# Both layernorms by way of DRAM and VectorE's block turns instead of TensorE's transposes

## The chip, the cores and the metric

The kernel runs on one core of one Trainium2 chip. The metric is the time of one execution in device microseconds; runs of the same kernel are compared by their medians.

## What is computed

There are eight batches of 1024 tokens, each with a width of 512, and a context of 1024 rows with a width of 384. Each batch passes through two blocks, both gated with tanh of a scalar and added to x:

```python
x = x + tanh(g_xattn) * xattn(layernorm(x), ctx)     # 8 heads of 64, softmax over 1024 context rows
x = x + tanh(g_ffn)   * ffn(layernorm(x))            # 16 heads of 32, self attention

# ffn, per head
q_norm = q / norm(q);  q_scaled = (q_norm + query_embedding) * softplus(temperature)
h = softmax(q_scaled @ k.T / sqrt(32)) @ v
# gates: softmax of 15 routed logits, the top 3 kept; softmax of 2 shared logits
out = (h * sum_of_gates) @ Wp.T + bp

def layernorm(x):      # over the 512 of a row, without weights
    return (x - mean(x)) / sqrt(var(x) + 1e-5)
```

Both layernorms work along a row of x. The projections after them contract over these 512, so TensorE needs the normalised rows turned: features on the partitions, tokens along the free axis.

## The kernel before

Everything is in float32, but for copies of queries and keys in bfloat16 from which the row maxima are taken. A batch is 8 tiles of 128 tokens. A chunk is 128 of the 512 columns of the heads: 2 heads in the first attention and 4 in the second, so each attention has 4 chunks. A chunk's life is: project q and k (`pq`, `pk`, and in the second attention `pn` for the norm of q), take the row maxima (TensorE writes `pm`, VectorE reduces to `mx`), turn the maxima (`pr`), cast them on ScalarE (`rows`), copy them with four small DMAs into one row (`sh`), and then go step by step through the keys: scores `sc` on TensorE, exp on ScalarE into `e`, pair sums of `e` on GpSimd (L483), sums of the pairs on VectorE (L496) or, where VectorE is late, on TensorE (`sum`, L516), and values `av` on TensorE.

The order on TensorE, ScalarE, VectorE and GpSimd is written by hand: a small planner in the kernel keeps a clock `at` for TensorE, VectorE and GpSimd, adds assumed costs with `pe(...)`, `dve(...)` and `pool(...)`, and decides from it which work goes between the steps of an attention. `attend` runs one chunk's attention, and takes as fillers what belongs to other chunks or to the next batch. The order of DMAs on the queue of SyncE (SP) is left to the framework's scheduler; the queue is served in that order, and a DMA that waits holds those behind it.

The layernorms are these steps of it:

- Batch 0's first layernorm stands at the kernel's start (`norm` and `transposed`).
- For the next batch, `stats1` (L750) is a filler of the attention over the last chunk of the first attention: for each of 8 tiles it loads x (`xs`) and takes mean and variance on VectorE (`bn_stats`, `bn_aggr`), and after the eighth it makes the reciprocal deviations of all tiles at once on ScalarE (Ln, Exp).
- `ln1` (L759) is a filler of the attention over chunk 2 of the second attention: it loads x again (`xn`), scales it in place on ScalarE (L203), transposes it with four matmuls against the identity into PSUM (`pt`, L218), and ScalarE copies that to `y1T` (L219).
- `between` (L944) stands between the two attentions: for each tile the output projection of the first attention (`po`, 16 matmuls of the program), the gated residual on VectorE (L955), statistics, Ln, Exp and the scaled row (`norm`, L205), and, two tiles behind, the same transposes and copy into `y2T`. GpSimd adds the bias of the last projection to x (L961). The last two transposes stand behind the first three quarters of the next chunk's q projection. That projection and the one of k are taken in halves of 512 tokens; the second half reads tiles 4 to 7.

The tag `wa` has four buffers of a tile (128x512), which loaded rows and scaled rows share.

Of the kernel before, what the change touches and what calls it, by code (L numbers as in the profile page):

```python
# [10 lines left out]
F32 = mybir.dt.float32  # L11
# [5 lines left out]
P = 128  # L17
# [4 lines left out]
def tile_gated_block(  # L22
# [38 lines left out]
    nc = tc.nc  # L61
    B, N, D = x.shape
    DC = cT.shape[1]
    NT = N // P
    ND = D // P
# [14 lines left out]
    epool = ctx.enter_context(tc.tile_pool(name="epool", bufs=9))  # L80
    work = ctx.enter_context(tc.tile_pool(name="work", bufs=2))
    small = ctx.enter_context(tc.tile_pool(name="small", bufs=1))
    ps_gen = ctx.enter_context(tc.tile_pool(name="ps_gen", bufs=3, space=bass.MemoryType.PSUM))
    ps_sc = ctx.enter_context(tc.tile_pool(name="ps_sc", bufs=2, space=bass.MemoryType.PSUM))
    ps_av = ctx.enter_context(tc.tile_pool(name="ps_av", bufs=1, space=bass.MemoryType.PSUM))
# [17 lines left out]
    def load_w(ap, name):  # L103

        k, m = ap.shape
        w = wpool.tile([P, k // P, m], F32, tag="wbig", name=name)
        nc.sync.dma_start(out=w, in_=ap.rearrange("(c p) m -> p c m", p=P))
        return w
# [79 lines left out]
    def inverse(rs, mv):  # L188

        nc.scalar.activation(rs, mv[..., 1:2], AF.Ln, bias=eps_c)  # L190
        nc.scalar.activation(mv[..., 1:2], rs, AF.Exp, scale=-0.5)
        nc.vector.scalar_tensor_tensor(
            mv[..., 0:1], mv[..., 0:1], -1.0, mv[..., 1:2], ALU.mult, ALU.mult
        )

    def stats(mv, xt, key):
        st = small.tile([P, 6], F32, tag="st", name=f"st_{key}", bufs=2)
        nc.vector.bn_stats(st, xt)
        nc.vector.bn_aggr(mv, st)
        dve(1000)  # L200

    def scaled(xn, xt, mv):
        nc.scalar.activation(xn, xt, AF.Identity, bias=mv[:, 0:1], scale=mv[:, 1:2])  # L203

    def norm(xt, key):  # L205

        mv = small.tile([P, 2], F32, tag="mv", name=f"mv_{key}", bufs=2)
        rs = small.tile([P, 1], F32, tag="rs", name=f"rs_{key}", bufs=2)
        xn = work.tile([P, D], F32, tag="wa", name=f"xn_{key}", bufs=4)
        stats(mv, xt, key)  # L210
        inverse(rs, mv)
        scaled(xn, xt, mv)
        return xn

    def transposed(xn, yT, t, key):
        pt = ps_gen.tile([P, ND, P], F32, tag="gen", name=f"pt_{key}_{t}")
        for c in range(ND):
            nc.tensor.transpose(pt[:, c, :], xn[:, ts(c, P)], ident)  # L218
        nc.scalar.copy(yT[:, :, ts(t, P)], pt)  # L219
        pe(TR)  # L220
# [3 lines left out]
    WIDE, MM, PAIR, FOUR, TR, SUM, EXP = 700, 950, 300, 350, 800, 1000, 2100  # L224

    part = [False]
# [7 lines left out]
    def pe(ns):  # L234
        at["PE"] += ns

    def dve(ns):
        at["DVE"] = max(at["DVE"], at["PE"]) + ns

    def pool(ns):  # L240
        at["POOL"] = max(at["POOL"], at["PE"]) + ns
# [18 lines left out]
    def gen(name):  # L260
        return ps_gen.tile([P, H], F32, tag="gen", name=name)
# [394 lines left out]
    def beside(a, b, n=1):  # L656

        while a or b:
            for g in [a] * n + [b]:
                if g and next(g, "end") == "end":  # L660
                    a, b = (None if g is a else a), (None if g is b else b)
                elif g:
                    yield

    def run(g, ns):

        end = at["PE"] + ns
        while g and at["PE"] < end:
            if next(g[0], "end") == "end":
                g.pop(0)  # L670
# [74 lines left out]
    def load_rows(st, t, key):  # L745
        xt = work.tile([P, D], F32, tag="wa", name=f"{key}_{st.b}_{t}", bufs=4)
        nc.sync.dma_start(out=xt, in_=x[st.b, ts(t, P), :])
        return xt

    def stats1(st):  # L750

        st.mv = small.tile([P, NT, 2], F32, tag="mv1", name=f"mv1_{st.b}")
        for t in range(NT):
            stats(st.mv[:, t, :], load_rows(st, t, "xs"), f"1_{st.b}_{t}")
            yield
        rs = small.tile([P, NT, 1], F32, tag="rs1", name=f"rs1_{st.b}")
        inverse(rs, st.mv)

    def ln1(st, xts):  # L759

        st.yT = big.tile([P, ND, N], F32, tag="yT", name=f"y1T_{st.b}")
        scaled(xts[0], xts[0], st.mv[:, 0, :])
        for t in range(NT):
            if t + 1 < NT:
                scaled(xts[t + 1], xts[t + 1], st.mv[:, t + 1, :])
            if t + 2 < NT:
                xts.append(load_rows(st, t + 2, "xn"))
            if t == 0:
                yield
            transposed(xts[t], st.yT, t, f"1_{st.b}")  # L770
            yield

    def begin(b):
# [47 lines left out]
    def out_project(ps, hT, w, t):  # L821
        part = hT[t // NQ]
        return product(ps, lambda k: part[:, k, ts(t % NQ, P)], lambda k: w[:, k, :], ND)
# [120 lines left out]
    def between(st, nxt):  # L944

        b = st.b
        wo = st.w
        st.yT = big.tile([P, ND, N], F32, tag="yT", name=f"y2T_{b}")
        xns = {}

        def output(t):
            ps = gen(f"po1_{b}_{t}")
            for _ in out_project(ps, st.hT, wo, t):
                pass
            nc.vector.scalar_tensor_tensor(st.x[t], ps, tg1, st.x[t], ALU.mult, ALU.add)  # L955
            xns[t] = norm(st.x[t], f"2_{b}_{t}")
            dve(900)

        def turn(t):
            transposed(xns.pop(t), st.yT, t, f"2_{b}")  # L960
            nc.gpsimd.tensor_tensor(st.x[t], st.x[t], bp_b, ALU.add)  # L961
            pool(1270)

        one, two, three = st.chunks[2][0:3]
        one.loads()
        two.loads()
        for t in range(NT):
            output(t)
            due(at["PE"] if t + 1 < NQ else 1e12)
            if t > 1:  # L970
                turn(t - 2)
        st.wv = load_w(wv2, f"wv2_{b}")
        st.v2 = new_v(st, 2)
        fill = [one.project(st)]
        run(fill, 3 * MM)
        three.loads()
        turn(NT - 2)
        turn(NT - 1)
        run(fill, 1e9)
        fill = [two.project(st), v2(st)]  # L980
        if nxt:
            fill.append(fetch(nxt, wv1, "wv1"))
        fill.append(three.project(st))
        run(fill, 2 * MM)
        pace(one, fill, two, 64 * MM)
        run(fill, 1e9)
        new_hT(st, 2)
# [25 lines left out]
    st = begin(0)  # L1013
    one = st.chunks[1]
# [8 lines left out]
    fill, values = [one[0].project(st)], [v1(st)]  # L1023
    run(fill, 2 * NDC * MM)
    xn = None
    for t in range(NT):
        was, xn = xn, norm(st.x[t], f"1_0_{t}")
# [9 lines left out]
    fill = values + [one[1].project(st), one[2].project(st)]  # L1037
# [4 lines left out]
    for b in range(B):  # L1042
        nxt = begin(b + 1) if b + 1 < B else None
        st.v = st.v1
        new_hT(st, 1)
        one, two = st.chunks[1], st.chunks[2]

        fill, cost = [], 0
        if prev:
            one[2].loads()  # L1050
            fill, cost = [finish(prev, one[2].project(st))], 58 * MM
        attend(one[0], one[1], b == 0, fill, cost, one[1], one[2], rate=1.4)
        one[3].loads()
        st.w = load_w(wo1, f"wo1_{b}")
        attend(one[1], one[2], False, [one[3].project(st)], 15 * MM, one[2], one[3], rate=3)
        if nxt:
            nxt.ct = load_ctx(b + 1)
        attend(one[2], one[3], False, [residual(st)], 2800, one[3])
        attend(one[3], None, False, [stats1(nxt)] if nxt else [], 2800)
        between(st, nxt)  # L1060

        st.v = st.v2
        fill = [v1(nxt)] if nxt else []
        attend(two[0], two[1], True, fill, 24.5 * MM, two[1], two[2], rate=1)
        two[3].loads()
        rows = [load_rows(nxt, t, "xn") for t in range(2)] if nxt else []
        attend(two[1], two[2], False, [two[3].project(st)], 18.5 * MM, two[2], two[3], rate=1.6 if nxt else 3)
        st.w = load_w(wp2, f"wp2_{b}")
        if nxt:
            one = nxt.chunks[1]  # L1070
            one[0].loads()
            fill = [ln1(nxt, rows), one[0].project(nxt)]
            next(fill[0])
            attend(two[2], two[3], False, fill, 8 * 2100 + 14.5 * MM, two[3], one[0], rate=1, least=2100)
            one[1].loads()
            attend(two[3], one[0], False, [one[1].project(nxt)], 14.5 * MM, one[0], one[1], rate=1)
            prev, st = st, nxt
        else:
            attend(two[2], two[3], False, [], 0, two[3])
            fill = [finish(st)]  # L1080
            attend(two[3], None, False, fill, 20 * MM, since=0.5)
# [37 lines left out]
```

## Time and profile before

| | us |
|---|---|
| median of 3 runs | 4942.89 |
| the runs | 4939.43 to 4947.75 |
| the profiled execution | 4944.07 |
| its span (first to last instruction) | 4942.1 |

| engine | busy, us | share of the span |
|---|---|---|
| TensorE (PE) | 4805.1 | 97% |
| VectorE (DVE) | 3097.8 | 63% |
| GpSimd (POOL) | 2578.9 | 52% |
| ScalarE (ACT) | 2307.4 | 47% |

The mean granted TensorE clock is 0.993. The batches follow each other in a fixed rhythm: the second batch's output loop (`between`) begins at 866.46 us, the third's at 1476.91 and the fourth's at 2088.43, so a batch takes about 611 us.

The lines from the profile are read like this. A row of the groups has the line, engine and operation, then output from inputs by the program's names, the shapes and the number of instructions; after the bar come the busy time in us (the union, so that matmuls that overlap count once) and the mean length of one in ns; after the second bar, how long the engine was idle just before these, and what ended that. A row of the timeline has the start and the length in us, then the same names; the bracket is the idle time before it and its releaser. The profile counts a float32 matmul as two instructions, a transpose as one. PEld is the loading of weights, which runs beside PE; SPq is the queue of SyncE.

### The profile page before, as it was taken

How to read it: one execution, taken by the hardware profiler on the slowest of the kernel's cores; microseconds unless marked ns; L12 is line 12 of the kernel's file. 1: busy time of each engine (PE TensorE's matmuls, PEld its weight loads, DVE VectorE, ACT ScalarE, POOL GpSimd, SP SyncE). 2: the span in 40 equal slices, each digit the busy share in tenths (PEclk: the TensorE clock that was granted, in tenths of full speed). 3: DMA queues.
4: the chain of work that ended last, by engine and by line, in shares of the span. 5: the costliest groups of instructions: out<-in, count | busy, mean ns of one | idle time of the engine just before them, and what ended most of it. 6: DMA issues, size and time to landing. Idle time of an engine off the chain costs nothing.

```text
span 4942.1 us, 83648 instructions
## 1 busy us (share of the span) xinstructions
PE 4805.1 (97%) x35564; PEld 1457.5 (29%) x35564; DVE 3097.8 (63%) x4126; ACT 2307.4 (47%) x3029; POOL 2578.9 (52%) x1346
## 2 busy tenths in 40 slices
PE   9999999999999999999999999999999999999998
PEld 2222332223322233222332223322233222333232
DVE  4557665577555765557655577555775557754664
ACT  3435634356343563436634356343662436624364
POOL 1635646366363663636636366363663636636474
PEclk9999999999999999999999999999999999999999
DMA  2010010100101001010020100101001010010000
GB/s 80 27 33 15 26 50 26 33 17 23 50 26 37 14 23 51 26 37 14 24 65 12 37 14 24 65 12 37 14 24 67 9 37 18 13 52 1 27 1 18
DMA packets 126277, 145.14 MB, mean 29 GB/s; under 512 B 14544, under 2 KB 75984, under 8 KB 125904
## 3 DMA queue, kind: packets, MB, share of 16 engines
q1 hardware_dynamic: 125616, 139.81, 8.9%
q8 instruction: 278, 4.55, 0.4%
q14 instruction: 95, 0.78, 0.1%
q10 hardware_dynamic: 288, 0.00, 0.0%
HBM read 122.47 MB, written 16.78 MB: 28 GB/s over the span
## 4 chain that ended last, share of the span: by engine, by line
PE 81%; DVE 11%; issue 2%; ACT 2%; POOL 2%; DMA 0%; SPq 0%; DVEq 0%; ACTq 0%; POOLq 0%
PE sc L467 21%; PE av L565 18%; PE po L249 8%; PE pq L249 8%; PE pm L380 7%; PE pk L249 7%; PE pv L249 5%; DVE mx L404 4%; DVE mx L421 4%; PE sum L516 3%; DVE e L496 3%; POOL e L483 1%; PE pt L218 1%; PE pn L249 1%; ACT e L478 1%
## 5 line engine op out<-in xcount | busy, mean ns | idle before, releaser
L483 POOL TENSOR_TENSOR e<-e,e 128x1024 f32<-128x1024 f32 x764 | 1864.3, 2455 | 1135.2 <-PE av L565 659.7
L478 ACT ACTIVATE e<-sc 128x1024 f32<-128x1024 f32 x1536 | 1491.4, 1021 | 1199.1 <-PE sc L467 1151.8
L421 DVE TENSOR_REDUCE mx<-pm 128x1 f32<-128x512 f32 x2332 | 1489.9, 685 | 792.2 <-PE pm L380 751.2
L467 PE MATMUL sc<-q,k 32*128 32x512 f32 (+1 forms) x6144 | 1189.9, 604 | 0.0
L496 DVE TENSOR_TENSOR e<-e,e 128x1024 f32<-128x1024 f32 x455 | 874.2, 1935 | 335.2 <-POOL e L483 334.3
L565 PE MATMUL av<-e,v 128*32 128x512 f32 (+1 forms) x6144 | 1083.0, 614 | 0.0
L380 PE MATMUL pm<-kb,qb 32*128 32x512 bf16 (+1 forms) x3072 | 625.7, 383 | 58.6 <-DVE mx L421 25.9
L404 DVE TENSOR_REDUCE mx<-pm 128x2 f32<-128x1024 f32 x370 | 427.7, 1219 | 292.5 <-PE pm L380 292.5
L467 PEld LDWEIGHTS sc<-q,k 32*128 32x128 f32 (+1 forms) x6144 | 478.5, 189 | 198.5 <-issue 186.6
L467 PE MATMUL sc<-sh,ones_b 1*128 1x512 bf16 x3072 | 406.9, 385 | 32.3 <-ACT e L478 17.3
L380 PEld LDWEIGHTS <-qb 32*128 32x128 bf16 (+1 forms) x3072 | 151.7, 92 | 918.5 <-issue 903.9
L565 PEld LDWEIGHTS av<-e,v 128*32 128x32 f32 (+1 forms) x6144 | 193.9, 117 | 609.1 <-issue 589.7
L249 PE MATMUL pq<-y1T,wq 128*32 128x512 f32 (+1 forms) x1568 | 247.1, 600 | 6.5 <-ACT r L540 2.6
L249 PE MATMUL pq<-y2T,wq 128*32 128x512 f32 x2048 | 247.5, 601 | 2.8 <-ACT rn L347 2.8
L249 PE MATMUL pv<-wv,y2T 128*32 128x512 f32 x2048 | 241.3, 597 | 0.0
L249 PE MATMUL pk<-y2T,wk 128*32 128x512 f32 x2048 | 241.2, 594 | 0.0
L249 PE MATMUL po<-wp,h2T 128*64 128x512 f32 (+1 forms) x1152 | 231.1, 595 | 0.0
L249 PE MATMUL po<-wo,h1T 128*32 128x512 f32 x2048 | 229.7, 594 | 1.2 <-ACT y2T L219 0.8
L467 PEld LDWEIGHTS <-ones_b 1*128 1x128 bf16 x3072 | 104.6, 91 | 394.2 <-issue 378.0
L249 PE MATMUL pk<-ctx,wk 128*32 128x512 f32 (+1 forms) x1176 | 189.8, 606 | 19.5 <-DMA ctx<-in_ctx 6.0
L349 POOL TENSOR_TENSOR qq<-qq,rn 128x512 f32<-128x512 f32 x64 | 89.3, 1396 | 223.3 <-ACT rn L348 215.6
L552 POOL TENSOR_TENSOR h1T<-h1T,r 128x512 f32<-128x512 f32 x64 | 81.2, 1269 | 221.5 <-ACT r L541 134.6
(109 smaller groups left out, 2985.9 us busy)
## 6 DMA issues: line engine op xcount, KB each, us to landing
x<-in_x SPq DMA_DIRECT2D x64, 256.0 KB
out<-x SPq DMA_DIRECT2D x64, 256.0 KB
xs<-in_x SPq DMA_DIRECT2D x56, 256.0 KB
xn<-in_x SPq DMA_DIRECT2D x56, 256.0 KB
ctx<-in_ctx SPq DMA_DIRECT2D x7, 1536.0 KB
wq<-in_L_xattn_Wq SPq DMA_DIRECT2D x32, 256.0 KB
wo<-in_L_xattn_Wo SPq DMA_DIRECT2D x8, 1024.0 KB
wk<-in_L_ffn_Wk SPq DMA_DIRECT2D x32, 256.0 KB
```

Of the source, the lines that this page charges most:

```text
L249: nc.tensor.matmul(ps[ts(j, w), :], lhsT=lhsT[:, ts(j, w)], rhs=rhs, start=start, stop=stop)
L349: nc.gpsimd.tensor_tensor(self.qq, self.qq, rn, ALU.mult)
L380: nc.tensor.matmul(ps, lhsT=self.qb[ts(i, width), ts(c, P)], rhs=self.kb[ts(i, width), ts(kh, H)], start=True, stop=True,)
L404: nc.vector.tensor_reduce(out, tiles[u], AX.X, ALU.max)
L421: nc.vector.tensor_reduce(mx[:, i * NT + c, kh : kh + 1], ps, AX.X, ALU.max)
L467: nc.tensor.matmul(pss[u][:, j % 2, :], lhsT=lhsT, rhs=rhs, start=(m == 0), stop=(m == 1))
L478: nc.scalar.activation(e[u], pss[u], AF.Exp)
L483: nc.gpsimd.tensor_tensor(one, one, two, ALU.add)
L496: nc.vector.tensor_tensor(accs[-1], accs[-1], a, ALU.add)
L516: nc.tensor.matmul(ps[ts(2 * u + j, self.width), :], lhsT=ones[:, 0 : self.width], rhs=acc[n][:, j, :], start=(n == 0), stop=(n == len(acc ...
L552: engine.tensor_tensor(hT, hT, r, ALU.mult)
L565: nc.tensor.matmul(self.av[ts(i, width), :], lhsT=st.v[:, kc, ts(self.c * self.nh + i, width)], rhs=e[j // 2][:, j % 2, :], start=(kc == 0 ...
```

## The change

The normalised rows no longer go through TensorE. `scaled` writes a row with its columns regrouped: the four blocks of 32 columns that belong on the same 32 partitions stand side by side. `put` stores that tile in DRAM (256 KB, one DMA). `get` loads it back with four DMAs, one for each group of 32 partitions, so that every 32 by 32 block lies on the partitions it belongs on (each piece is 512 bytes long). `turned` then has VectorE transpose all sixteen blocks in one instruction and write them to `y1T` or `y2T`.

For the first layernorm, `put1` takes the place of `stats1`: it is in the same attention, and does the whole normalisation there, with Ln, Exp and scaled row for each tile on ScalarE. `ln1` only loads (three tiles ahead) and turns; the second loading of x is gone. The filler's assumed cost goes from 2100 ns a tile to 300, and its steps now alternate with the steps of the next chunk's projection.

For the second layernorm, `between` stores each tile behind its output, loads it behind the next tile's output, and turns it three tiles behind instead of two. The last three turns stand between the first products of the next projection. The loaded tiles lie in `wa` and in two buffers that the attention uses for sums (`part`, `r`). Batch 0's first layernorm stays as it was.

```diff
+    far = ctx.enter_context(tc.tile_pool(name="far", bufs=1, space=bass.MemoryType.DRAM))
...
-    def norm(xt, key):
+    def norm(xt, key, apart=False):
...
-        scaled(xn, xt, mv)
+        if apart:
+            q = P // 32
+            scaled(
+                xn.rearrange("p (q c j) -> p q c j", q=q, c=ND),
+                xt.rearrange("p (c q j) -> p q c j", q=q, c=ND),
+                mv,
+            )
+        else:
+            scaled(xn, xt, mv)
         return xn
+
+    def put(xt, key, bufs):
+        y = far.tile([P, D], F32, tag=f"y{bufs}", name=f"y_{key}", bufs=bufs)
+        nc.sync.dma_start(out=y, in_=norm(xt, key, apart=True))
+        return y
+
+    def get(y, key, tag="wa"):
+        q = P // 32
+        xb = work.tile([P, D], F32, tag=tag, name=f"xb_{key}", bufs=4 if tag == "wa" else 1)
+        src = y.rearrange("(u i) (q f) -> q i u f", i=32, q=q)
+        for j in range(q):
+            nc.sync.dma_start(
+                out=xb[ts(j, 32), :].rearrange("i (u f) -> i u f", u=q), in_=src[j]
+            )
+        return xb
+
+    def turned(xb, yT, t):
+        nc.vector.transpose(
+            yT[:, :, ts(t, P)].rearrange("p c (u i) -> p u c i", i=32),
+            xb.rearrange("p (u c j) -> p u c j", c=ND, j=32),
+        )
+        dve(600)
...
-    def stats1(st):
-        st.mv = small.tile([P, NT, 2], F32, tag="mv1", name=f"mv1_{st.b}")
+    def put1(st):
+        st.far = []
         for t in range(NT):
-            stats(st.mv[:, t, :], load_rows(st, t, "xs"), f"1_{st.b}_{t}")
+            st.far.append(put(load_rows(st, t, "xs"), f"1_{st.b}_{t}", NT))
             yield
-        rs = small.tile([P, NT, 1], F32, tag="rs1", name=f"rs1_{st.b}")
-        inverse(rs, st.mv)
-    def ln1(st, xts):
+    def ln1(st):
+        xbs = []
+        def fetched():
+            t = len(xbs)
+            if t < NT:
+                xbs.append(get(st.far[t], f"1_{st.b}_{t}"))
+        for _ in range(3):
+            fetched()
+        yield
         st.yT = big.tile([P, ND, N], F32, tag="yT", name=f"y1T_{st.b}")
-        scaled(xts[0], xts[0], st.mv[:, 0, :])
         for t in range(NT):
-            if t + 1 < NT:
-                scaled(xts[t + 1], xts[t + 1], st.mv[:, t + 1, :])
-            if t + 2 < NT:
-                xts.append(load_rows(st, t + 2, "xn"))
-            if t == 0:
-                yield
-            transposed(xts[t], st.yT, t, f"1_{st.b}")
+            turned(xbs[t], st.yT, t)
+            fetched()
             yield
...
-        xns = {}
+        xns, xbs = {}, {}
...
-            xns[t] = norm(st.x[t], f"2_{b}_{t}")
+            xns[t] = put(st.x[t], f"2_{b}_{t}", 4)
...
-            transposed(xns.pop(t), st.yT, t, f"2_{b}")
+            turned(xbs.pop(t), st.yT, t)
...
+        tags = ("wa", "part", "wa", "r")
         for t in range(NT):
             output(t)
             due(at["PE"] if t + 1 < NQ else 1e12)
-            if t > 1:
-                turn(t - 2)
+            if t:
+                xbs[t - 1] = get(xns.pop(t - 1), f"2_{b}_{t - 1}", tags[t % 4])
+            if t > 2:
+                turn(t - 3)
+        xbs[NT - 1] = get(xns.pop(NT - 1), f"2_{b}_{NT - 1}", tags[0])
         st.wv = load_w(wv2, f"wv2_{b}")
         st.v2 = new_v(st, 2)
         fill = [one.project(st)]
-        run(fill, 3 * MM)
+        run(fill, 2 * MM)
         three.loads()
-        turn(NT - 2)
-        turn(NT - 1)
+        for t in range(NT - 3, NT):
+            turn(t)
+            run(fill, 3 * MM)
         run(fill, 1e9)
...
-        attend(one[3], None, False, [stats1(nxt)] if nxt else [], 2800)
+        attend(one[3], None, False, [put1(nxt)] if nxt else [], 2800)
...
-        rows = [load_rows(nxt, t, "xn") for t in range(2)] if nxt else []
...
-            fill = [ln1(nxt, rows), one[0].project(nxt)]
-            next(fill[0])
-            attend(two[2], two[3], False, fill, 8 * 2100 + 14.5 * MM, two[3], one[0], rate=1, least=2100)
+            turns = ln1(nxt)
+            next(turns)
+            fill = [beside(turns, one[0].project(nxt))]
+            attend(two[2], two[3], False, fill, NT * 300 + 14.5 * MM, two[3], one[0], rate=1)
```

## The prediction

> **What bounds the kernel now.** I read the page first: busy times, chain, clock.
>
> ```profile
> PE 4805.1 (97%) x35564; PEld 1457.5 (29%) x35564; DVE 3097.8 (63%) x4126; ACT 2307.4 (47%) x3029; POOL 2578.9 (52%) x1346
> ...
> PE 81%; DVE 11%; issue 2%; ACT 2%; POOL 2%; DMA 0%; SPq 0%; DVEq 0%; ACTq 0%; POOLq 0%
> ```
>
> TensorE is busy 97% and carries 81% of the chain; its clock row is 9s throughout. Only 4942.1 - 4805.1 = 137 us of the span are free of matmuls. So a change gains where it takes matmuls out, and loses where it makes the matmul queue wait. Next, the groups with shapes kept apart, for what is removed and for the nearest relative of what is added:
>
> ```profile
> L218 PE MATMUL pt<-ident,xn 128*128 128x128 f32 x512 | 83.6, 286 | 8.3 <-DVE mx L421 3.5 <-ACT part L529 2.7 <-ACT xn L203 1.7
> ...
> L198 DVE BATCH_NORM_STATS2 st<-xs 128x6 f32<-128x512 f32 x56 | 37.7, 673 | 0.0
> ...
> L219 ACT COPY y2T<-pt 128x512 f32<-128x512 f32 x64 | 36.5, 570 | 1.3
> ```
>
> All 512 transposes together are 83.6 us of PE; 480 go (the first layernorm of batch 0 keeps its 32). Then the timeline of three stages of one batch; here the second layernorm's output loop:
>
> ```profile
> 1476.91 10.51 PE L249 MATMUL po<-wo,h1T 128*32 128x512 f32 x96
> ...
> 1487.35 1.08 PE L516 MATMUL sum<-e,ones 128*64 128x512 f32 x4
> ...
> 1501.07 0.66 PE L218 MATMUL pt<-ident,xn 128*128 128x128 f32 x4
> ...
> 1501.65 3.64 PE L249 MATMUL po<-wo,h1T 128*32 128x512 f32 x32
> ...
> 1505.22 0.66 PE L218 MATMUL pt<-ident,xn 128*128 128x128 f32 x4
> ...
> 1509.52 0.75 DVE L955 SCALAR_TENSOR_TENSOR x<-po,tg,x 128x512 f32<-128x512 f32 x1 [1.70 <-PE po L249]
> ...
> 1512.01 0.81 ACT L203 ACTIVATE xn<-x,mv 128x512 f32<-128x512 f32 x1 [0.23 <-DVE mv L192]
> ```
>
> A tile with a transpose takes 1505.22 - 1501.07 = 4.15 us, without (1487.35 - 1476.91) / 3 = 3.48. From the residual add's start to the scaled row's end is 12.82 - 9.52 = 3.30 us. In the attention that hides the first layernorm's statistics:
>
> ```profile
> 1457.89 0.40 PE L467 MATMUL sc<-sh,ones_b 1*128 1x512 bf16 x4
> ...
> 1459.45 1.94 ACT L478 ACTIVATE e<-sc 128x1024 f32<-128x1024 f32 x2 [2.17 <-PE sc L467]
> ```
>
> ScalarE idles 2.17 us in a 4.11 us step here (1462.00 starts the next), and is done at 1461.39, 0.6 to 0.8 us before the next scores write the second tile that it read. That is all the room there is. Last, what a round trip costs (SyncE's queue), and what a late transfer costs:
>
> ```profile
> 693.22 0.34 SPq L894 DMA_DIRECT2D out<-x  x1
> 695.23 0.33 SPq L89 DMA_DIRECT2D x<-in_x  x1
> ```
>
> ```profile
> 511.76 2.70 SPq L436 DMA_DIRECT2D sh<-rows  x4
> ...
> 514.87 0.39 PE L467 MATMUL sc<-sh,ones_b 1*128 1x512 bf16 x1 [0.65 <-DMA sh<-rows]
> ...
> 515.54 0.37 PE L467 MATMUL sc<-sh,ones_b 1*128 1x512 bf16 x1 [0.29 <-DMA sh<-rows]
> ```
>
> The load that waits for the store is issued 2.01 us after it: a 256 KB store lands in that. The fourth of the small copies starts at 511.76 + 3 x 0.68 = 513.80 and PE goes on at 515.54: 1.74 us from issue to use. The profiled execution took 4944.07 us (span 4942.1 and 2.0 around it), 1.2 over the median of 4942.89.
>
> **The change, stage by stage.** *Second layernorm (8 batches).* Out of the PE order go two transposes behind the loop (1512.68 to 1513.93, 1.25 us) and six in it (0.67 each). VectorE gets 8 block turns a batch. None is in the trace. Nearest row: the statistics, 128x512 f32 out of SBUF, 0.67 to 0.69; below, 0.48 (the plain tensor-scalar over 128x512, L161); above, 1.4, if a 4-byte element passes twice. I take 0.7. VectorE's tile is then 2.46 us (add, statistics, aggregate, 0.6 of waiting for ScalarE's Ln and Exp, the product) + 0.7 = 3.2, inside 3.48: it keeps up, just. At 1.4 it would not.
>
> The new wait is at the end. PE ends the eighth tile at 1476.91 + 8 x 3.48 + 1.0 (the sum) = 1505.75. The next projections need 7.89 us (9.14 from 1509.97 to the second half's start at 1519.11, less 1.25) until they read tiles 4 to 7: 1513.64. The last tile: add at 1505.89, scaled row at +3.30 = 1509.19, store issued at 1509.3, landed at 1511.3. In SP's order four loads of tile 6 stand between, then four of tile 7. Issue of one: 0.38 for the weights' three-dimensional loads, 0.68 for the small copies; I take 0.5. Tile 7 starts at 1511.65, its fourth at 1513.15, landed at 1514.9, turned at 1515.7. PE waits 2.1 us where it waited for nothing; the second half starts 1519.11 - 1515.7 = 3.4 earlier than now. At 0.38 it is 4.1, at 0.68 it is 2.2. Times 8: **-27 us** (-33 to -17). Waiting behind the last turn on VectorE are the first maxima, needed some 15 us later. The weights wv2 and wk, wq of the third chunk move behind these transfers on SP by some 5 us; they are read over 15 us later. POOL's bias add (L961, 1.28) moves one tile later; nobody waits for x.
>
> Two rules of the Trainium skill speak against this. Row: four small copies take 2.70 us of SP, one 256 KB load 0.33. "DMA: Bandwidth & Descriptors", rules for kernel authors, says to coalesce, transfers under 64 KB being mostly overhead, and not to split by partitions, as both halves use the same engines. By it one load would do 3 x 0.5 = 1.5 us better at this place, or 12 us over 8 batches; the sum keeps the four as they are, since the queue is what I priced. "VectorE: DVE Perf Modes", the three transpose paths, gives 311 ns for 128x128 bf16 on VectorE and says 32x32 blocks alone are turned, its rules sending 128x128 to TensorE. From 311 ns, at one element a cycle of 0.96 GHz, 384 more columns add 400 ns: 0.71 us, an estimate for bf16. It agrees with the row's 0.7; the advice does not decide, since here PE is the engine that is short.
>
> *First layernorm's turning (7 batches, in the attention of chunk 2).* Each transpose moves the next matmul by 0.59 (527.96 to 528.55); 8 are 4.7, and two waits in front of them (0.50 and 0.39) are 0.9. Given back: the instruction order of the changed program has 8 more row-sum matmuls a batch in that chunk (28 fewer adds on VectorE in all); eight take 508.31 - 506.48 = 1.83. And the maxima's transpose of the last chunk now stands one step before its scores: between them only 1.0 + 2.05 + 1.0 of PE work, the pattern of the 514.87 rows, which waited 0.94 with a pair of maxima more in between; I take 1.3. Net 5.6 - 1.8 - 1.3 = 2.5; times 7: **-17 us**. On SP the copies of those maxima stand behind the loads of tiles 4 to 7, which wait for turns 0 to 3, and behind two weights, which wait for the next chunk's projections; in the order all of these end before the maxima do, so I cost that at nothing, and at the time from the maxima to the last such projection if it is not so. The blocks are fetched three ahead, some 10 us before use, and VectorE has its 8 turns (5.6 us) against 4 adds fewer (about 8).
>
> *First layernorm's statistics (7 batches, the last chunk of attention 1).* So far VectorE alone worked here. Now each tile puts Ln, Exp and the scaled row into ScalarE's order: 0.29 + 0.20 + 0.81 and 0.35 of waiting for VectorE, 1.65 us, between the exps. Behind them are the exps, and PE waits for those. Room is about 2.1 us a step less the copies that are already there, but two tiles stand together twice (0 and 1; 4 and 5). Tile 0's Ln cannot start before VectorE's aggregate at 1449.45; two tiles end at 1452.95 instead of exps at 1450.37. These end at 1454.9, PE wants to write at 1454.0: 1.0. The next step has a sum's Ln and Exp and tile 2: 0.65. Tiles 4 and 5 with the copy of h1T: 1.6. Together 3.3 a batch, **+23 us** (1 to 8 a batch, +7 to +56: below, if VectorE reaches the statistics early; above, if its adds, now behind the product that waits for ScalarE, release e late). The loads xs are one tile ahead on SP, behind the store of the tile before.
>
> Elsewhere nothing changes; 120 copies less on ScalarE (69 us) are off the path. The 56 second loads of x go, 120 stores and 480 loads come; the queue's 8.9% of the DMA engines leaves room for them.
>
> Sum: -27 - 17 + 23 = -21 us. 4944.07 - 21 = 4923; against the median, 4922.
>
> **Rivals.** *All hidden:* 8 x (6 x 0.67 + 1.25) + 7 x 5.6 = 81 us, 4862. For it: 2.17 us of idle ScalarE. Against: the last tile's round trip, which nothing covers.
>
> *ScalarE's order decides (slower):* exps queue behind layernorm rows that wait for VectorE, whose adds wait for POOL (L496 waits 334 us for it in the whole run). It outweighs the gain from (27 + 17) / 7 = 6.3 us a batch on, 0.8 a tile; at 10 a batch the sum is +26: 4969. For it: the 0.6 to 0.8 us of room per step. Against: VectorE is half idle there.
>
> *The turn costs 1.4:* VectorE then needs 3.9 for PE's 3.48; five turns fall 2 us behind, the last adds 0.7: 2.7 x 8 = +22, which cancels the gain: 4943.
>
> **Numbers.** Partial gain, 4895 to 4933: 0.44. All hidden: 0.07. ScalarE's order: 0.27. Cancelled within 0.2% (9.9 us, about what measurement tells from none): 0.13. Other losses, above all transfers that land later than the rows say: 0.09. Faster 0.51, same 0.13, slower 0.36. The range leaves out a tenth at each end: 4880 to 4985; the likeliest case's own is 4895 to 4933.
>
> **What would show it.** After: 32 pt matmuls; block turns near 0.7; PE idle of about 2 us once a batch before pq or pk of the second half; "PE sc <- ACT e" up from 17 us by some 20; "sc <- DMA sh" up by some 9. Wrong, if turns take over 1 us, if that idle is over 5, or if exps wait for Ln by more than 6 us a batch.

## The result: slower by 0.55%, and the profile after

| | before | after |
|---|---|---|
| median, us | 4943.8 (4939.4 to 4947.8) | 4971.4 (4967.6 to 4972.7) |
| ratio, 95% interval | | 1.0055 (1.0037 to 1.0072) |
| span of the profiled execution | 4942.1 | 4969.5 |
| mean granted TensorE clock | 0.993 | 0.986 |

The forecast was 4922; the change costs 28 us where 21 were to be gained. The page after, busy times and chain:

```profile
PE 4781.6 (96%) x35196; PEld 1434.4 (29%) x35196; DVE 3142.1 (63%) x4274; ACT 2276.6 (46%) x3014; POOL 2571.2 (52%) x1346
...
PE 73%; DVE 14%; ACT 4%; issue 4%; POOL 3%; DMA 1%; SPq 1%; ACTq 0%; DVEq 0%; POOLq 0%
```

TensorE is only 23.5 us less busy, though 480 transposes (79 us) went. The chain now passes through VectorE, ScalarE and GpSimd for 21% of the span instead of 15%. In the groups, the transposes are gone as planned, the new block turns cost what was assumed, and in one small group, which I had passed over, the mean has doubled:

```profile
L252 PE MATMUL pt<-ident,xn 128*128 128x128 f32 x32 | 5.0, 285 | 1.7 <-ACT xn L204 1.7
...
L243 DVE STREAM_TRANSPOSE y2T<-xb 128x512 f32<-128x512 f32 x64 | 45.3, 708 | 39.6 <-DMA xb<-y 39.1
L243 DVE STREAM_TRANSPOSE y1T<-xb 128x512 f32<-128x512 f32 x56 | 37.7, 692 | 0.0
...
L193 DVE SCALAR_TENSOR_TENSOR mv<-mv 128x1 f32<-128x1 f32 x128 | 72.9, 570 | 145.5 <-ACT mv L192 145.5
```

The same product before (line 192 there), of one column a partition, and of eight where `stats1` made it for all tiles at once:

```profile
L192 DVE SCALAR_TENSOR_TENSOR mv<-mv 128x1 f32<-128x1 f32 x72 | 20.0, 277 | 56.5 <-ACT mv L191 56.5
L192 DVE SCALAR_TENSOR_TENSOR mv<-mv 128x8 f32<-128x8 f32 x7 | 13.2, 1888 | 5.4 <-ACT mv L191 5.4
```

What TensorE waits for (engine and line, released by, total us, times, longest), after:

```profile
PE sc L501 <- ACT e L512: 45.5, 45, 2.9
...
PE pq L283 <- DVE y2T L243: 19.8, 9, 3.1
PE sc L501 <- DMA sh<-rows: 11.4, 22, 1.8
```

and before:

```profile
PE sc L467 <- ACT e L478: 17.3, 18, 2.9
PE sc L467 <- DMA sh<-rows: 11.6, 21, 1.8
```

Two waits are new: 28 us more for exps, all in the `put1` stage (29.0 us there, where there was none), and 20 us for the last block turn. Together they are 48 us, and the row sums that moved from VectorE to TensorE 14 more; that is less than the 79 us of transposes that went. The rest is in the clock. I cut both traces by stage, at the first scores of each chunk and the first output product of each batch, and added up, by stage, its length, the idle time of TensorE in it, and the clock that was not granted (one minus the granted share, times how long):

| stage, all batches, after minus before | length, us | TensorE idle | clock not granted |
|---|---|---|---|
| last chunk of the first attention (`put1`) | +58.4 | +29.2 | +20.5 |
| between the attentions | -13.6 | +18.4 | +10.2 |
| second attention, chunk 1 | +9.8 | +4.0 | +5.1 |
| second attention, chunk 2 (`ln1`) | -31.9 | -3.6 | -3.4 |
| all else | +4.7 | +2.8 | +1.4 |
| sum | +27.4 | +50.8 | +33.8 |

The clock that was not granted grew by 33.8 us, which is more than the whole loss. Not all of it counts, since TensorE waits for others in part of these stretches (run 3). How the clock is lost shows at the end of the stage between the attentions. The timeline there:

```profile
1522.66 0.34 SPq L227 DMA_DIRECT2D y<-xn  x1
1523.11 3.72 SPq L236 DMA_DIRECT2D xb<-y  x8
...
1526.10 1.07 PE L283 MATMUL pn<-rn,hsum 128*32 128x512 f32 x8
...
1528.73 0.71 DVE L243 STREAM_TRANSPOSE y2T<-xb 128x512 f32<-128x512 f32 x1 [1.38 <-DMA xb<-y]
...
1529.59 5.34 PE L283 MATMUL pq<-y2T,wq 128*32 128x512 f32 x32 [2.43 <-DVE y2T L243]
1534.72 3.64 PE L283 MATMUL pk<-y2T,wk 128*32 128x512 f32 x32
```

SyncE's queue issues the store of the eighth tile at 1522.66 us, and behind it the eight loads of the seventh and the eighth tile in one row until 1526.83. The wait of 2.43 us for the eighth tile's round trip is the one that was forecast (2.1). But the 32 matmuls behind it take 5.34 us, and the same number of the next group 3.64. The windows of this place (PE busy, then the other engines, PEclk, DMA share, GB/s) say why:

```profile
1527.01:1530.43 3.42, 0.99 (x12) 0.34 (x12) 1.05 (x2) 1.71 (x4) 1.47 (x2) 1.00 0.79 226
1530.43:1533.84 3.41, 3.41 (x20) 1.08 (x16) 0.00 (x0) 0.37 (x1) 0.00 (x0) 0.50 0.83 257
1533.84:1537.25 3.41, 3.41 (x36) 1.25 (x32) 0.00 (x0) 0.69 (x1) 1.04 (x1) 1.00 0.32 93
```

A window of 3.41 us in which TensorE was busy for 0.99 us only is followed by one at half clock (0.50), and that costs 1.7 us more. The profile before has such stretches too: 18 of them, 69.3 us long, so 34.7 us of clock not granted; the tenths of the page (a row of 9s) hide them. After, there are 37, with 68.5 us not granted.

In the `put1` stage the timeline shows what ScalarE, with the exps behind it, waits for:

```profile
2074.39 2.35 POOL L517 TENSOR_TENSOR e<-e,e 128x1024 f32<-128x1024 f32 x1 [1.40 <-ACT mv L192]
2074.42 2.33 DVE L193 SCALAR_TENSOR_TENSOR mv<-mv 128x1 f32<-128x1 f32 x1 [0.59 <-ACT mv L192]
...
2076.79 0.81 ACT L204 ACTIVATE xn<-xs,mv 128x512 f32<-128x512 f32 x1 [2.40 <-DVE mv L193]
2077.51 1.92 ACT L512 ACTIVATE e<-sc 128x1024 f32<-128x1024 f32 x2
...
2078.56 0.39 PE L501 MATMUL sc<-sh,ones_b 1*128 1x512 bf16 x2 [2.64 <-ACT e L512]
...
2079.80 3.65 PE L501 MATMUL sc<-q,k 64*128 64x512 f32 x8
```

VectorE's product of one number a partition takes 2.33 us, as long as GpSimd's add of 1024 columns beside it. ScalarE waits 2.40 us for it, the exps wait for ScalarE, TensorE 2.64 us for the exps, and its next scores take 3.65 us (1.99 a step earlier), as the clock was 0.50 from 2079.98 to 2083.39 us.

### The profile page after: what moved, and what is told of

Read it like the earlier page. It is cut to its first block, busy times and chain, and to the rows that moved or that the text cites. A ratio compares the mean times of both kernels' runs of the same rounds, so it can differ in the third digit from the quotient of the medians.

```text
span 4969.5 us, 84000 instructions
## 1 busy us (share of the span) xinstructions
PE 4781.6 (96%) x35196; PEld 1434.4 (29%) x35196; DVE 3142.1 (63%) x4274; ACT 2276.6 (46%) x3014; POOL 2571.2 (52%) x1346
## 4 chain that ended last, share of the span: by engine, by line
PE 73%; DVE 14%; ACT 4%; issue 4%; POOL 3%; DMA 1%; SPq 1%; ACTq 0%; DVEq 0%; POOLq 0%
PE sc L501 18%; PE av L599 15%; PE po L283 9%; PE pq L283 7%; PE pm L414 7%; PE pk L283 6%; PE pv L283 5%; DVE mx L438 4%; DVE mx L455 4%; DVE e L530 3%; PE sum L550 3%; POOL e L517 3%; ACT e L512 2%; DVE mv L193 1%; PE pn L283 1%
## 5 line engine op out<-in xcount | busy, mean ns | idle before, releaser
L501 PE MATMUL sc<-q,k 32*128 32x512 f32 (+1 forms) x6144 | 1206.1, 608 | 0.0
L530 DVE TENSOR_TENSOR e<-e,e 128x1024 f32<-128x1024 f32 x427 | 802.2, 1889 | 262.0 <-POOL e L517 260.9
L501 PE MATMUL sc<-sh,ones_b 1*128 1x512 bf16 x3072 | 420.4, 385 | 61.2 <-ACT e L512 45.5
L283 PE MATMUL pq<-y2T,wq 128*32 128x512 f32 x2048 | 259.5, 628 | 22.6 <-DVE y2T L243 19.8
L550 PE MATMUL sum<-e,ones 128*32 128x512 f32 (+1 forms) x1380 | 210.2, 596 | 0.3 <-POOL e L517 0.2
```

What stands on the lines that cost most here:

```text
L283: nc.tensor.matmul(ps[ts(j, w), :], lhsT=lhsT[:, ts(j, w)], rhs=rhs, start=start, stop=stop)
L501: nc.tensor.matmul(pss[u][:, j % 2, :], lhsT=lhsT, rhs=rhs, start=(m == 0), stop=(m == 1))
L530: nc.vector.tensor_tensor(accs[-1], accs[-1], a, ALU.add)
L550: nc.tensor.matmul(ps[ts(2 * u + j, self.width), :], lhsT=ones[:, 0 : self.width], rhs=acc[n][:, j, :], start=(n == 0), stop=(n == len(acc ...
```

## The experiments

The theory: the loss is in the `put1` stage, where a chain ScalarE, VectorE, ScalarE stands between the exps; and each gap of TensorE of some 2 us costs its own length and half clock behind it. The rivals are in the expectations. Each kernel was timed in five rounds beside the kernel before; ratios are against that. Stage numbers are from one profiled execution of each kernel, as sums over the batches against before; such an execution lies up to 10 us from its kernel's median.

**1. Only the second layernorm changed.** The first keeps `stats1` and the old `ln1`; the diff is that of `between`, `norm`, `put`, `get` and `turned` alone.

> Only the second layernorm takes the new way; the first stays as it was before. Stage theory (each stage's cost is its own, a gap of over 2 us before the second half of the projections, plus half clock for 3.4 us behind most of these gaps): the stage between the attentions is 1.5 us a batch shorter where the clock drops and 3 us where it does not, 12 to 25 us in all, so 4919 to 4932 us. The prediction's own term was -27: 4917, with no change of the clock. Rival (the stages share queues, so neither part alone shows its share): within 5 us of 4944.

Measured 4934.1 us, ratio 0.9979 (0.9971 to 0.9987). The stage between the attentions is 17.0 us shorter, with 17.3 us of new idle time and 8.5 us of clock not granted; in batches without half clock it is 2.9 to 3.3 shorter, in the others 1.4 to 1.6. Chunk 1 of the second attention, whose work is as before, is 8.4 longer. The stage came out as the theory has it; the total lies 2 us above its range, which the theory doesn't explain, since it has nothing for chunk 1.

**2. Only the first layernorm changed.** `put1` and the new `ln1`; `between` as before.

> Only the first layernorm takes the new way; the stage between the attentions stays as it was before. Stage theory: +58 in the last chunk of the first attention (7 batches of 9.0 us, less in the first), -32 in chunk 2 of the second attention, about +5 elsewhere: 4967 to 4985 us, slower than before by about 31. The prediction's terms were +23 - 17 = +6: 4950.

Measured 4975.3, ratio 1.0060 (1.0047 to 1.0073). The stages read +59.5 for `put1`, -31.5 for the turning, -0.2 between the attentions, +7.2 in chunks 0, 1 and 3 of the second attention. The first layernorm loses, the second gains. By the stages the two parts hardly disturb each other; by the medians -10 and +31 us make +22, where both together cost 28, with an interval from 18 to 36.

**3. Useless matmuls in the gaps.**

```diff
+    def idle(key, n):
+
+        ps = gen(f"idle_{key}")
+        for _ in range(n):
+            nc.tensor.matmul(ps, lhsT=ident, rhs=bo_b, start=True, stop=True)
...
+            if (self.kind, self.c, step) == (1, ND - 1, (0, 3)) and self.b + 1 < B:
+                idle(f"1_{self.b}", 3)
...
             turn(t)
-            run(fill, 3 * MM)
+            if t + 1 == NT:
+                run(fill, MM / 2)
+                idle(f"2_{b}", 2)
+            run(fill, (2 if t + 1 == NT else 3) * MM)
```

> The changed kernel with useless float32 matmuls of 128x128 by 128x512 put where TensorE waits: two before the second half of the projections between the attentions (8 batches) and three before the fourth step of the scores of the last chunk of the first attention (7 batches); nobody reads their results. They fit inside the waits (about 0.85 us each; waits of 2.2 to 3.1 and 2.6 us). Clock theory (a 3.4 us window with over about 1.2 us of idle TensorE is followed by one at half clock, which costs 1.7 us): the waits' own length stays, but six drops of the clock between the attentions and seven at the fourth step go, 13 x 1.7 = 22 us, so about 4949 us, faster by adding work; granted clock back to about 0.990. Rival (a gap costs its own length and no more): 4971, or up to 10 more where the useless matmuls overrun the wait.

Measured 4950.7, ratio 1.0010 (1.0002 to 1.0019): 21 us faster than the changed kernel, by doing more. Its profiled execution (4941.1, so 10 us below the median) has 21 stretches at half clock instead of 37. The same place as above, timeline and windows of this kernel:

```profile
1523.48 1.07 PE L283 MATMUL pn<-rn,hsum 128*32 128x512 f32 x8
1524.48 1.98 PE L301 MATMUL idle<-bo_b,ident 128*128 128x512 f32 x4
1526.81 3.64 PE L283 MATMUL pq<-y2T,wq 128*32 128x512 f32 x32 [0.35 <-DVE y2T L243]
```

```profile
1524.16:1527.57 3.41, 3.06 (x16) 1.02 (x16) 1.22 (x2) 1.70 (x4) 1.72 (x2) 1.00 0.69 186
1527.57:1530.99 3.42, 3.42 (x36) 1.26 (x32) 0.00 (x0) 1.04 (x2) 0.00 (x0) 1.00 0.70 243
```

The second half starts 3.33 us behind `pn` (3.49 above), so the round trip is as long as it was; but its 32 matmuls take 3.64 us and not 5.34. Between the attentions no clock is lost any more, and the stage is 25.0 us shorter than before instead of 13.6. That shows that the gap's second price is the clock. In the `put1` stage the lost clock falls from 20.5 to 6.8 us, but the stage only from +58.4 to +52.0: there ScalarE is late, and a faster TensorE waits for it.

**4. The eighth tile of the second layernorm transposed on TensorE.**

```diff
-            xns[t] = put(st.x[t], f"2_{b}_{t}", 4)
+            if t + 1 < NT:
+                xns[t] = put(st.x[t], f"2_{b}_{t}", 4)
+            else:
+                xns[t] = norm(st.x[t], f"2_{b}_{t}")
...
-            turned(xbs.pop(t), st.yT, t)
+            if t + 1 < NT:
+                turned(xbs.pop(t), st.yT, t)
+            else:
+                transposed(xns.pop(t), st.yT, t, f"2_{b}")
...
-        xbs[NT - 1] = get(xns.pop(NT - 1), f"2_{b}_{NT - 1}", tags[0])
```

> The changed kernel, but the eighth tile of the second layernorm is transposed on TensorE as before (four transposes behind the first half of the projections, copied by ScalarE); the other seven go through DRAM. Round trip theory: the wait before the second half (2.2 to 3.1 us a batch) and the drop of the clock behind it (1.7 us in 6 of 8 batches) go, the transposes cost 0.67: 8 x (2.4 - 0.67) + 6 x 1.7 = 24 us, so about 4947 us. Rival (the seventh tile's round trip is as late, because the queue's loads and not the tile's own chain set the end): the wait stays over 1 us and the time over 4960.

Measured 4945.1, ratio 0.9997 (0.9989 to 1.0006). The wait for `y2T` is gone, the stage is 39.4 us shorter than before (4.9 in every batch), and no clock is lost in it. Seven tiles through DRAM are covered; the eighth alone was not.

**5. In `put1`, the product on ScalarE.**

```diff
         nc.scalar.activation(mv[..., 1:2], rs, AF.Exp, scale=-0.5)
+        if alone:
+            nc.scalar.activation(rs, mv[:, 0:1], AF.Identity, scale=mv[:, 1:2])
+            nc.scalar.mul(mv[:, 0:1], rs, -1.0)
+            return
...
```

> The changed kernel, but in the last chunk of the first attention the product of mean and reciprocal deviation of a tile is made on ScalarE (two one-column operations of some 0.2 us each) instead of on VectorE, so that ScalarE no longer waits for VectorE between its Exp and the scaled row. Theory of the crossing (VectorE's one-column product takes up to 2.3 us while GpSimd adds, and ScalarE, with the exps behind it, waits for that: 81 us in 56 tiles, 1.45 each): a tile is 1.45 - 0.4 = 1 us shorter where it counts, the 2.6 us wait of TensorE at the fourth step goes, and the stage loses 3 to 5 us a batch instead of 9: 4930 to 4945. Rival (ScalarE has too much work there, whoever it waits for): 0.4 us more for each of 8 tiles and 7 batches, 4971 to 4990.

Measured 4949.3, ratio 1.0008 (0.9999 to 1.0016): 22 us faster than the changed kernel, with two more instructions a tile on ScalarE and one less on VectorE. The stage falls from 9.0 to 5.9 us a batch in most batches; that and the time lie above what was expected (3 to 5, and 4930 to 4945). The expectation had counted too much wait: its 1.45 a tile puts the 81 us that all of the kernel's scaled rows wait for the product on the 56 tiles of this stage, where it is 56.9 us, 1.02 a tile. The same two tiles in the new timeline:

```profile
2065.71 0.81 ACT L208 ACTIVATE xn<-xs,mv 128x512 f32<-128x512 f32 x1
2066.43 1.92 ACT L516 ACTIVATE e<-sc 128x1024 f32<-128x1024 f32 x2
2067.48 0.39 PE L505 MATMUL sc<-sh,ones_b 1*128 1x512 bf16 x2 [0.44 <-ACT e L516]
```

The 2.64 us are 0.44. The crossing to VectorE and back was a third of the stage's loss, 19.9 of 58.4 us. Of the 38.5 that stay, 10.2 are clock; run 6 shows how much hangs on ScalarE's row.

**6. In `put1`, the scaled row on VectorE.** ScalarE keeps Ln and Exp.

```diff
...
+            nc.scalar.activation(rs, mv[:, 1:2], AF.Ln, bias=eps_c)
+            nc.scalar.activation(rs, rs, AF.Exp, scale=-0.5)
...
+            nc.vector.tensor_scalar(
+                xn.rearrange("p (q c j) -> p q c j", q=q, c=ND),
+                xt.rearrange("p (c q j) -> p q c j", q=q, c=ND),
+                mv[:, 0:1], rs, ALU.subtract, ALU.mult,
+            )
...
```

> The changed kernel, but in the last chunk of the first attention VectorE makes the scaled row (subtract the mean, multiply by the reciprocal deviation, in one operation); ScalarE keeps only Ln and Exp, and waits for VectorE only before them. Theory of the crossing, and that of ScalarE's load: both go, the stage loses 0 to 2 us a batch instead of 9: 4910 to 4925. Rival (VectorE becomes late with its adds, of which the freeing of e, and so the exps, depend): the stage loses 7 us or more, over 4955.

Measured 4926.2, ratio 0.9965 (0.9952 to 0.9978). The stage costs 2.1 us in most batches, 16.5 in all; that and the time lie just above what was expected. The group of the new row:

```profile
L216 DVE TENSOR_SCALAR xn<-xs,mv,rs 128x512 f32<-128x512 f32 x56 | 73.9, 1320 | 47.2 <-ACT rs L214 47.2
```

The row takes 1.32 us in the mean, and 0.55 in the one case that met no GpSimd work. That is slower in the mean than on ScalarE (0.81), and still the better place: the exps, which are on ScalarE, don't stand behind it, and the rival (VectorE late with its adds, 7 us or more) did not come.

**7. The scaled rows later.** Statistics as before; loads, scaled rows and stores are a filler of chunk 1 of the second attention.

```diff
...
+            xt = load_rows(st, t, "xr")
+            scaled(
+                xn.rearrange("p (q c j) -> p q c j", q=q, c=ND),
+                xt.rearrange("p (c q j) -> p q c j", q=q, c=ND),
+                st.mv[:, t, :],
+            )
+            nc.sync.dma_start(out=y, in_=xn)
...
-        attend(two[1], two[2], False, [two[3].project(st)], 18.5 * MM, ...)
+        attend(two[1], two[2], False, [beside(rows, two[3].project(st))], 18.5 * MM, ...)
```

> The changed kernel, but in the last chunk of the first attention VectorE alone takes the statistics, with one Ln and Exp for all eight tiles, as before; x is loaded again, and the scaled rows (0.81 us each on ScalarE, without any wait for VectorE) and their stores stand between the steps of chunk 1 of the second attention. Theory (what costs is the chain of ScalarE and VectorE between the exps of a stage that TensorE cannot wait in): the stage is back at 36.3 us (-58 in all), chunk 1 costs 0 to 2 us a batch more, chunk 2 keeps its 32 us: 4913 to 4930. Rival (the rows are late in any attention): chunk 1 loses 6 us a batch or more, over 4950.

Measured 4989.2, ratio 1.0085 (1.0072 to 1.0098): a miss. The `put1` stage is back at 36.3 us, as expected, but chunk 1 costs 28.9 us more than before and chunk 2, which gained 32, loses 36. The windows of one chunk 2:

```profile
1192.00:1206.00 14.00, 13.37 (x115) 4.15 (x110) 10.45 (x18) 8.94 (x10) 8.54 (x5) 1.00 0.07 20
1206.00:1226.50 20.50, 15.48 (x55) 3.94 (x57) 9.50 (x15) 4.82 (x6) 3.25 (x3) 0.58 0.01 2
```

and its timeline:

```profile
1203.88 9.13 DVE L455 TENSOR_REDUCE mx<-pm 128x1 f32<-128x512 f32 x15
...
1207.69 0.37 PE L414 MATMUL pm<-kb,qb 32*128 32x512 bf16 x1 [0.23 <-DVE mx L455]
1208.29 0.37 PE L414 MATMUL pm<-kb,qb 32*128 32x512 bf16 x1 [0.23 <-DVE mx L455]
```

Each row took a step of its own between the projection's, so the projection of the last chunk ended late, and its maxima came in one burst of 14 matmuls with nothing beside them, at VectorE's pace. In most batches TensorE then stayed at half clock for five windows of 3.4 us, beyond the end of the burst. The theory that the planner's order was at fault, and not the rows, is tested by run 11.

**8. The rows later, and the eighth tile on TensorE** (7 and 4 together).

> The two repairs together: scaled rows of the first layernorm in chunk 1 of the second attention, eighth tile of the second layernorm transposed on TensorE. If the stages are independent: the time of the rows in chunk 1 less 26 us, 4887 to 4904 us, 40 to 56 us under the kernel before. Rival (drops of the clock move with the phase of the 3.4 us windows and eat the gain): over 4915.

Measured 4966.3, ratio 1.0040 (1.0028 to 1.0053). The expectation assumed that 7 would hold, and missed with it. The run still shows that the repair of 4 stands by itself: 22.9 us under 7, with the stage between the attentions at -39.5 again.

**9. Only the second layernorm changed, with its eighth tile on TensorE** (1 and 4).

> Only the second layernorm takes the new way, and of it the eighth tile is transposed on TensorE; the first layernorm stays as it was before. If the stages are independent: -39 us between the attentions (-4.9 a batch, measured with the eighth tile on TensorE), nothing else but the clock's phase in chunk 1 of the second attention (-3 to +10): 4902 to 4915 us. Rival (part of the gain hangs on the first layernorm's way): over 4925.

Measured 4904.3, ratio 0.9925 (0.9912 to 0.9939); the stage at -39.4, all other stages together at about 0. This is what the part between the attentions is worth without its last wait.

**10. Rows on VectorE, eighth tile on TensorE** (6 and 4).

> The whole change with the first layernorm's scaled rows on VectorE and the eighth tile of the second on TensorE. Sum of the stages as measured apart: -39 between the attentions, +16 in the last chunk of the first attention, -32 in chunk 2 of the second, 0 to +15 in chunks 1 and 3: 4889 to 4905 us. Rival (the clock's phase eats it): over 4915.

Measured 4900.1, ratio 0.9914 (0.9901 to 0.9928). The sums of the stages hold: -39.2, +14.4 and -29.7. Against 9 the first layernorm's way brings only 4 us, and the two intervals overlap: its turning gains 29.7, its rows take 14.4, and chunks 1 and 3 another 16, 10 of them clock.

**11. The rows later, without a step of their own, and the eighth tile on TensorE.** The diff is against run 8.

```diff
+    def along(a, b):
+        for _ in a:
+            if b and next(b, "end") == "end":
+                b = None
+            yield
+        while b and next(b, "end") != "end":
+            pass
...
-        attend(two[1], two[2], False, [beside(rows, two[3].project(st))], 18.5 * MM, ...)
+        attend(two[1], two[2], False, [along(two[3].project(st), rows)], 18.5 * MM, ...)
```

> The repair with the rows in chunk 1 of the second attention again, with the eighth tile on TensorE, but now each row stands beside a step of the next chunk's projection in the same step and no longer takes a step of its own. Theory (in the first try the rows took eight steps from the projection, so that the last chunk's maxima came late and in one burst of 17 us at half clock, in chunk 2): chunk 2 is back at -32 instead of +36, the stage of the statistics stays at 36.3, chunk 1 costs 0 to 3 us a batch: 4873 to 4895. Rival (the rows on ScalarE are themselves late): chunk 1 or 2 stays over 4 us a batch above before, over 4910.

Measured 4882.5, ratio 0.9881 (0.9868 to 0.9895), 1.2% under the kernel before and 1.8% under the changed one. Its page and TensorE's wait for exps:

```profile
PE 4751.3 (97%) x35228; PEld 1421.4 (29%) x35228; DVE 3109.1 (64%) x4217; ACT 2256.9 (46%) x2924; POOL 2565.6 (52%) x1346
```

```profile
PE sc L501 <- ACT e L512: 14.9, 18, 1.2
```

`put1`'s old place costs +0.2 us, the rows in chunk 1 +1.3, the stage between -39.4, chunk 2 -25.3, chunk 3 +12.3 with 13.8 us of clock not granted, for which no run gives the cause (this profiled execution lies 8 us above the median). Nothing but the order of the fillers differs from run 8, which is 84 us slower: the rows are not too much for ScalarE, only where they stood was wrong.

## Why the prediction was wrong, step by step

- *Second layernorm, -27:* measured -13.6. Turn, queue and wait were right: a turn takes 0.69 to 0.71 us (0.7 by the row, 0.71 by the estimate from the Trainium skill, "VectorE: DVE Perf Modes", "The three transpose paths"), the wait 2.43 us in the batch above and some 2.5 in the mean (19.8 us over the batches), where 2.1 were forecast. In the two batches without half clock the stage is 3.2 and 2.6 us shorter, where 3.4 were forecast. The step that failed is the price of the wait: "PE waits 2.1 us where it waited for nothing" was booked at its own length. Six batches paid 1.7 us more, 10.2 in all, as run 3 shows; some 3 more are the wait's own length. What one load a tile instead of four would bring, as the rule that the prediction cites has it, stays open: the trace shows the queue issuing the eight loads of the last two tiles without a pause, 0.47 us each, but no run loads a tile with one.
- *First layernorm's statistics, +23:* measured +58.4. The mechanism was right, exps behind rows that wait for VectorE, the size was not. The mis-sized term is "0.35 of waiting for VectorE": the scaled rows of this stage waited 56.9 us for the product, 1.02 each and up to 2.4. Run 5 takes it out: 19.9 us. Rows off ScalarE: 22.0 more (run 6). All of the change out of the stage: the last 16.5 (run 11). Within these, up to 20.5 us were clock, for which the sum had no term. The rest of the sum was about right: in run 5, with 0.5 us of ScalarE in the place of the wait, the stage loses 5.9 us a batch, 1.7 of it clock, and the other 4.2 lie near the 3.3 that were forecast with 0.35.
- *Turning, -17:* measured -31.9. The 1.3 us a batch for a late `sh` did not come: TensorE waits 11.4 us in all for `sh`, as against 11.6, and most of it where it did before, in front of the first scores of chunk 2 (7.9 us, 8.5 before). In front of the last chunk's scores, where the forecast had put it, it waits 2.5 us in all (2.2 before). Without it the sum is 7 x 3.8 = 27; of the rest, 3.4 us are clock that the trace before happened to lose in this chunk.
- *Elsewhere nothing changes:* measured +14.5, 6.5 of it clock. Chunk 1 of the second attention reads +9.8 in the changed kernel and -2.7 in run 3, which has the same order of instructions there: its gap of 2.0 us, which stands there in the kernel before too, may fall differently into the windows. Besides, a second wait of 1.13 us in front of a `pm` comes in 3 of the 8 batches before, in 6 after and in 1 of run 3; what brings it stays open. Of chunk 3 a lengthening of 0.4 us a batch stays unexplained.
- *The rival "ScalarE's order decides"* named the sign, the place and the time (4969 at 10 us a batch; the stage lost 9.0 in most batches). It had 0.27. That its total met 4971 so closely is in part luck: it adds +70 to -44, and measured were +58.4, -45.5 and +14.5 elsewhere. And of its chain the wait for VectorE came, but not for the adds that it named; the product itself was long. Against it stood only that "VectorE is half idle there"; idle time of an engine says nothing on how long its next small instruction takes. The profile before did say it, in this very stage, where one product for all eight tiles stood at the end. The seven of eight columns took 1.89 us each, all beside GpSimd's adds (shown above). Of the 72 of one column, nine met GpSimd work and took 1.10 us in the mean, the others 0.16; their common mean of 0.28 hides both.
- *What would show it:* the 32 transposes left, the turns near 0.7 and the idle time of about 2 us before the second half all came. The wait for exps rose by 28 us, not 20, and the one for `sh` not at all, where 9 were named. The stage with the exps lost 9.0 us a batch, beyond the mark of 6 that stood for wrong.

## What to carry to other kernels

Price a new gap of the busiest engine at its length and at what its clock does behind it, and read the granted clock in windows of a few microseconds, not in tenths over the whole span. A small operation that crosses engines in the middle of a stream of exps is priced by what its engine can be blocked by, so put such work where nobody's next instruction waits, or keep it on one engine. A round trip through DRAM was free for seven tiles of eight; let the last one take the short way.

## What the runs showed of the hardware

The half clock comes in windows of 3.413 us on a fixed grid: in every trace the starts of these windows lie at multiples of 3.413 us from one another, to 0.01 us. I counted the idle time of TensorE in each window of the thirteen traces, and whether the next window was at half clock:

| TensorE idle in a window of 3.413 us | next at half clock |
|---|---|
| under 0.6 us | 86 of 17916 |
| 0.6 to 1.2 | 44 of 495 |
| 1.2 to 2.2 | 220 of 280 |
| over 2.2 | 61 of 61 |

Of the 86 in the first row, 73 windows were at half clock already, as in the long stretches of run 7; only 13 were drops from the full clock.

The Trainium skill, "TensorE: Matmul & The Clock Gate", Part 1, gives the window (3413 ns, free-running), which agrees; its closing table asks for no idle gaps over about 3 us, and one idle window. By that rule the 2.4 us gaps here would cost nothing more; the measurement decides, and over 2.2 us of idle in a window were enough each time. The fixed grid fits with the differences between batches: in run 1 the stage between the attentions is 3.3 us shorter in one batch and 1.5 in another, with the same work and one window at half clock between them. What exactly is counted is open, since windows between 0.6 and 2.2 us go both ways.

A product of one column on VectorE takes 0.16 us in the 70 cases of the changed kernel that meet no GpSimd work, and 1.07 in the mean (up to 2.34) in the 58 that overlap it. Each of the 58 ends 0.01 to 0.02 us after the GpSimd instruction that it met. VectorE's adds of two tiles of 1024 columns lengthen too, 1.21 us alone and 2.26 in the mean beside GpSimd; statistics (0.69) and block turns (0.70), with one input, take the same in both cases. The Trainium skill, "SBUF — State Buffer", section "SBUF: two separate sides", says of the port pair that VectorE and GpSimd share that it is an exclusive lock for the whole instruction, which a VectorE operation with two SBUF inputs needs when GpSimd's reads SBUF. The traces agree in which of these operations wait and until when; the port itself they don't show. Two input tiles are not needed for it: the scaled row of run 6, from one tile and two columns, takes 0.55 us alone and 1.33 in the mean beside GpSimd. I had priced the product at its mean of before, when no ScalarE with exps behind it waited for it in this stage.
